# Layer 2's image attention output: fp32r products with high and low terms stacked along K instead of float32 products

## The chip, the core and the metric

The kernel runs on one core of one Trainium2 chip. The core has a matrix engine (PE), a vector engine (DVE), a scalar engine (ACT), a general engine (POOL) and a queue that issues transfers (SP); each works through its own instructions in order and waits for the others by semaphores. Sixteen DMA engines carry the transfers. The metric is the device time of one execution in microseconds, the median of several runs. Lower is better.

## The reference

Two layers of cross attention with two branches, applied one after the other to 16 sequences of 256 positions with 320 channels (20 heads of 16). Each layer attends to 252 (layer 2) or 77 (layer 1) text tokens and, beside them, to image tokens. The part that matters here is the image branch of layer 2, which has four image tokens per sequence:

```python
k_ip = heads(ip_ehs @ W_k_ip)
v_ip = heads(ip_ehs @ W_v_ip)
attn_scores = jnp.einsum('bhsd,bhnd->bhsn', q, k_ip) * attn_scale
qsem = _l2norm(jnp.einsum('bhst,bte->bhse', probs_t, text_ehs))
sem = jnp.einsum('bhse,bne->bhsn', qsem, _l2norm(ip_ehs))
probs_ip = jax.nn.softmax(attn_scores + SEM_SCALE * sem, axis=-1)
probs_ip = probs_ip * spatial_mask[None, None, :, None]
ip_out = jnp.einsum('bhsn,bhnd->bhsd', probs_ip, v_ip)
...
out = text_out + IP_SCALE * ip_out
out = out @ W_out + b_out
out = out + residual
```

The change touches `ip_out`: per sequence and head, 256 x 4 probabilities times 4 x 16 values, in float32 accuracy.

## The kernel before

The kernel runs 160 slots: 80 for layer 1, then 80 for layer 2 (`NS` = 80). A slot handles one group of four heads of one sequence ("batch"), so five slots are a batch. Work that is not attention (projections, softmax of the image branch, output projection, loading) is written as tasks, Python generators whose steps carry due times counted in slots; after certain points of a slot (`slot1` yields 0.33, 0.67 and 1.0) all steps whose time has come are issued, ordered by time and then by the order of definition. This order fixes PE's instruction stream: PE is pinned, so its queue is exactly what the program issues. The other engines and SP are ordered by a planner, which takes ready instructions, earlier-issued ones first, and inserts the semaphores. A few instructions are tied by hand: `queued` places the two operations that split the query input (L593, L594, tile `hq`) behind the last instruction of attention issued before them on ACT and POOL.

In a slot of layer 2, `both1` makes the scores of the slot after next (L891, tile S) and the transposed scores of this slot (L885, tile T); ACT takes the exponential (L905). `attend1` sums values by the probabilities (L945) and the norms (L955). `rounded1` splits the probabilities into a high part on ACT (L923) and a low part on POOL (L924); `norm1` multiplies the high part by the text tokens' Gram matrix on PE (L933) and the result by the low part's tile on DVE (L934). `norm1` has four calls per slot, of 4, 3, 4 and 3 products; tasks are issued after the first, after the third and after the fourth.

When a batch's five groups are through, task `i1` (`image_softmax`) forms the image probabilities on [128 x 160] tiles (partitions are query positions, the free axis is 8 blocks x 5 groups x 4 tokens): an inverse square root by a power on POOL (L1021), scaling and adding (L1024, L1026), the maximum, the exponential (L1033), the sum, and the normalisation (L1039, L1041). L1041 writes into a zero-padded tile `pip` [128 x 8 x 32]; DVE transposes it in 32x32 blocks to `pT` (L1048). The values stand in DRAM (`vipd`), are loaded to all 32-row blocks of `vb`, and are multiplied with a 128 x 384 0/1 mask `bmask`, so that each column of `vb` holds only its own head's group (L1049). Task `c1` (`close1`) multiplies: three float32 products of 128 x 128 by 128 x 256 (L1058), each added on DVE to the gathered text output `hT` (L1059). Then `finish` splits `hT` for the output projection (L593 to L595, tile `ho`), projects it (L605, L608) and adds bias and residual (L841, L845). The last batch's softmax runs in two parts: four groups early (task `i1a`), the fifth after the last slot.

fp32r is a 32-bit type whose products leave one record in the trace where float32 products leave two; the kernel treats it as rounded, and keeps accuracy by splitting an operand: high = the value rounded to fp32r, low = value - high rounded to fp32r, and summing high x high, high x low and low x high (`prod`, L243). L1058, like L945 and L955, is in plain float32.

Line numbers in the profile are those of the kernel before. All DMAs issued by `dma` carry L83.

Of the kernel before, what the change touches and what calls it, by code (L numbers as in the profile page):

```python
# [49 lines left out]
def xattn2(  # L50
# [80 lines left out]
    vipd = dram.tile([BI, CP], F32, name="vipd")  # L131
# [301 lines left out]
    def weights1():  # L433
# [4 lines left out]
        hop = w1["hop"] = dram.tile([128, CP], F32, name="hop")  # L438
        dma(hop, bmask_d)
# [33 lines left out]
    def weights6():  # L473
# [5 lines left out]
        vip = buf("rawc", [128, 512], bufs=2, name="vip")[:BI, :CP]  # L479
        for m in range(3):  # L480
            ms = slice(m * 128, m * 128 + 128)
            vp = bank()[:BI, :128]
            prod(vp, lambda s, k: cip[:, s, k], lambda s, k: wvi1(s, k, ms), 4)
            nc.vector.tensor_copy(vip[:, ms], vp)
            yield
# [3 lines left out]
        w1["bmask"] = f(buf("kb", [128, CP], FR, name="bmask"))  # L489
        dma(w1["bmask"], w1["hop"])  # L490
        dma(vipd, vip)
# [14 lines left out]
    def weights3():  # L506
# [500 lines left out]
    def image_softmax(b, lo=0, hi=NG):  # L1007
# [15 lines left out]
        a = small(NIP, "a")  # L1023
# [16 lines left out]
        pi = w1["pip"]  # L1040
        pool.tensor_mul(by_group(pi), a, b4(z4))  # L1041
# [6 lines left out]
        nc.vector.transpose(pT, pi.rearrange("p f c -> p (f c)"))  # L1048
        nc.vector.tensor_mul(vb, vb, w1["bmask"])  # L1049
        return pT, vb  # L1050

    def close1(b):
        hT, (pT, bd) = results["gathered", 1, b], get("i1", b)

        def extra(hT):
            for p in range(3):
                ip = bank()[:, :S]
                mm(ip, bd[:, p * 128 : (p + 1) * 128], pT, start=True, stop=True)  # L1058
# [63 lines left out]
    def shifted(n, *times):  # L1122

        return [RAMP(n + t) for t in times]
# [17 lines left out]
    for b in range(B):  # L1142
# [4 lines left out]
        task(("i1", b), shifted(n, 6.67, 6.67, 6.67, 7.33, 7.33, 7.67, 7.67, 8, 8.33), lambda b=b: image_softmax(b, NG - 1 if b == B - 1 else 0), ("gathered", 1, b), ("taken", B + b - 1), *([("i1a",)] if b == B - 1 else []))  # L1147
        task(("c1", b), shifted(n + (1.67 if b > B - 3 else 0), 8.67, 8.67, 8.67, 8.67, 9, 10.33, 11.67, 12.67), lambda b=b: close1(b), ("i1", b), ("w4", 1))
# [156 lines left out]
```

## Time and profile before

| | |
|---|---|
| median of 3 runs | 1554.69 us (1552.39 to 1557.26) |
| span of the profiled execution, first to last instruction | 1550.2 us |
| layer 2's loop | from about 800 us to 1500 us, 50.36 us a batch |
| L1058 matrix products | 96 records of 379 ns (median), first at 817.1, last at 1538.1 us |
| L1041, L1048, L1049 | 473, 434 and 546 ns (median) |

How to read the lines below. Groups and timelines name a line of the kernel, the engine, the operation, the tiles written and read, the shape and the number of instructions. In brackets stands how long the engine was idle before it and for whom it waited. PEld is PE's loading of the stationary operand; it overlaps with the products. PE's records overlap each other, so the time that PE is held is read from the chain of waits or from the distance of starts, not from the mean of a record. A float32 product leaves two records, an fp32r product one. A window of the stage table gives start:end, length, then the busy time of PE, PEld, DVE, ACT and POOL with the number of instructions, the granted clock, the DMA share and GB/s.

### The profile page before, as it was taken

The page shows a single profiled execution, that of the slowest core. Times are in us where ns is not written, and L with a number is a line of the kernel's source. Part 1 is how long each engine was busy: PE and PEld are TensorE (multiplying, and loading weights), DVE is VectorE, ACT ScalarE, POOL GpSimd, SP SyncE. Part 2 cuts the span into 40 slices and gives each one's busy share as a digit, 9 for nine tenths or more (in the row PEclk, how much of TensorE's full clock was granted, in tenths as well). Part 3 has the DMA queues.
Part 4 walks back from the last instruction along what each step waited for, and adds up shares of the span by engine and source line. Part 5 has one row for each costly group of instructions (what it writes and reads, how often), then busy time and mean ns, then how long its engine had stood idle before and what let it go on. Part 6 is the DMA issues. An engine that isn't in the chain of part 4 may idle for free.

```text
span 1550.2 us, 36017 instructions
## 1 busy us (share of the span) xinstructions
PE 1449.5 (94%) x12726; PEld 1170.2 (75%) x12726; DVE 1219.9 (79%) x2687; ACT 873.5 (56%) x1941; POOL 1196.1 (77%) x1246
## 2 busy tenths in 40 slices
PE   6789999999999989878999999999999999999996
PEld 5678888878787878656777777777777777777764
DVE  6468787778777888878777887888888888788785
ACT  5345555656564644545666666566656665666562
POOL 4259797979896976778478798878887898779786
PEclk9899999999999999989999999999999999999998
DMA  6656666676766675765354344434444444434411
GB/s 210 195 182 175 209 191 207 188 221 190 218 191 201 192 205 153 196 186 172 97 135 129 104 125 127 123 111 140 110 114 126 125 116 119 135 108 99 119 32 36
DMA packets 228815, 233.04 MB, mean 150 GB/s; under 512 B 38410, under 2 KB 198508, under 8 KB 228620
## 3 DMA queue, kind: packets, MB, share of 16 engines
q1 hardware_dynamic: 226428, 229.44, 52.0%
q8 instruction: 102, 1.67, 0.5%
q10 hardware_dynamic: 2208, 1.30, 0.3%
q14 instruction: 77, 0.63, 0.1%
HBM read 118.04 MB, written 77.10 MB: 126 GB/s over the span
## 4 chain that ended last, share of the span: by engine, by line
PE 34%; POOL 7%; DVE 7%; issue 2%; ACT 1%; DMA 1%; ACTq 1%; SPq 0%; DVEq 0%; POOLq 0%
PE X L933 11%; PE X L248 5%; POOL wt L924 5%; PE P L945 4%; PE P L955 3%; PE X L605 3%; PE T L885 2%; PE S L891 2%; DVE wt L934 2%; PE X L1058 1%; POOL hq L594 1%; DVE mn L893 1%; PE X L258 1%; DVE ho L595 1%; PE X L608 1%
## 5 line engine op out<-in xcount | busy, mean ns | idle before, releaser
L768 POOL TENSOR_TENSOR P<-P,rs 128x512 f32<-128x512 f32 x320 | 414.1, 1317 | 126.1 <-ACT P L765 125.6
L924 POOL TENSOR_TENSOR wt<-P,ctb 128x512 f32<-128x512 f32 x320 | 410.9, 1309 | 94.5 <-ACT ctb L923 91.8
L933 PE MATMUL X<-ctb,gm 128*128 128x512 f32 x1120 | 307.3, 404 | 6.0 <-DVE wt L934 5.9
L765 ACT ACTIVATE P<-T 128x512 f32<-128x512 f32 x320 | 175.9, 594 | 172.0 <-PE T L762 107.2
L934 DVE TENSOR_TENSOR wt<-X,wt 128x512 f32<-128x512 f32 x320 | 216.8, 682 | 53.3 <-PE X L933 47.8
L933 PEld LDWEIGHTS X<-ctb,gm 128*128 128x128 f32 x1120 | 196.5, 189 | 39.3 <-DVE wt L934 8.6
L905 ACT ACTIVATE P<-T 128x512 f32<-128x512 f32 x320 | 173.3, 594 | 78.8 <-PE T L885 74.6
L923 ACT ACTIVATE ctb<-P 128x512 fp32r<-128x512 f32 x320 | 187.2, 627 | 45.7 <-PE X L933 34.6
L893 DVE TENSOR_REDUCE mn<-S 128x4 fp32r<-128x1008 f32 x160 | 191.3, 1196 | 0.0
L740 DVE TENSOR_REDUCE mn<-S 128x4 fp32r<-128x716 f32 x160 | 142.3, 889 | 0.0
L795 PE MATMUL P<-P,vr 128*32 128x256 f32 x1920 | 126.9, 396 | 7.1 <-DVE tmp L812 6.7
L738 PE MATMUL S<-ks,qs 125*128 125x256 f32 x640 | 118.8, 309 | 9.2 <-DMA qs<-tph 4.6
L738 PEld LDWEIGHTS S<-ks,qs 125*128 125x128 f32 x640 | 89.3, 196 | 44.3 <-issue 23.7
L762 PE MATMUL T<-qs,ks 127*128 127x256 f32 x640 | 110.0, 293 | 4.5 <-DMA qs<-mt 2.3
L1021 POOL TENSOR_TENSOR r<-u,rs 128x40 f32<-128x40 f32 (+2 forms) x17 | 108.7, 6396 | 4.1 <-DVE u L1018 4.1
L739 DVE TENSOR_REDUCE mn<-S 128x4 fp32r<-128x308 f32 x160 | 74.2, 464 | 30.8 <-PE S L738 30.5
L762 PEld LDWEIGHTS T<-qs,ks 127*128 127x128 f32 x640 | 92.5, 198 | 7.7 <-ACT q L160 2.5
L795 PEld LDWEIGHTS P<-P,vr 128*32 128x32 f32 x1920 | 57.3, 113 | 48.6 <-issue 12.4
L806 DVE STREAM_TRANSPOSE nt<-P 128x512 f32<-128x512 f32 x80 | 56.9, 711 | 46.5 <-PE P L795 46.0
L605 PE MATMUL X<-hq,wE 128*128 128x256 f32 x512 | 80.3, 297 | 10.0 <-ACT hq L593 5.2
L945 PE MATMUL P<-P,v1t 128*32 128x256 f32 x1280 | 86.5, 388 | 0.2 <-DVE wt L934 0.2
L955 PE MATMUL P<-wt,zone 128*32 128x256 f32 x1280 | 85.3, 379 | 0.3 <-DVE wt L934 0.3
(231 smaller groups left out, 3018.0 us busy)
## 6 DMA issues: line engine op xcount, KB each, us to landing
qd<-q SPq DMA_DIRECT2D x96, 256.0 KB
qs<-tph SPq DMA_DIRECT2D x64, 308.0 KB
rawc<-in_cT_dram SPq DMA_DIRECT2D x60, 256.0 KB
qs<-qd SPq DMA_DIRECT2D x80, 192.0 KB
ks<-kd SPq DMA_DIRECT2D x80, 192.0 KB
ks<-kd SPq DMA_DIRECT2D x160, 96.0 KB
qs<-qd SPq DMA_DIRECT2D x160, 96.0 KB
kd<-kst SPq DMA_DIRECT2D x57, 256.0 KB
```

Of the source, the lines that this page charges most:

```text
L738: mm(sp[:, h], Q[: XROW + T0, h, t * 128 : (t + 1) * 128], K[: XROW + T0, h], start=True, stop=True)
L762: mm(st[p][:, j], K[:KS0, 2 * p + j, t * 128 : (t + 1) * 128], Q[:KS0, 2 * p + j], start=True, stop=True)
L765: exp = anchor(nc.scalar.activation(pt, st[p], AF.Exp, scale=SCALE))
L768: anchor(nc.gpsimd.tensor_mul(pt, pt, rs[:, t : t + 1].to_broadcast([128, 2, S])))
L795: mm(pv[32 * s : 32 * s + 32, o : o + S], v[:, vt, h : h + 32], P[k, s // 2][:, t, s % 2], start=vt < 2, stop=vt != 1,)
L893: anchor(nc.vector.tensor_reduce(maxes[k + 2][:, t], sp[:, :, :T1], axis=AX.X, op=ALU.max))
L905: anchor(nc.scalar.activation(P[k, u][:, t], st[u], AF.Exp, scale=SCALE))
L923: nc.scalar.activation(R[k, u][:, t], P[k, u][:, t], AF.Copy, scale=0.5)
L924: anchor(nc.gpsimd.tensor_sub(W[k, u][:, t], P[k, u][:, t], f(R[k, u][:, t])))
L933: mm(yp, gm[:, gb], R[k, u][:, kt], start=i == 0, stop=i == len(blocks[n]) - 1)
L934: nc.vector.tensor_mul(W[k, u][:, n], yp, W[k, u][:, n])
L945: mm(pv[32 * s : 32 * s + 32, :S], v[:, n, h : h + 32], P[k, s // 2][:, n, s % 2], start=n == 0, stop=n == 1 and not before,)
```

## The change

The probabilities and the values are both split in a high and a low part, and the three partial products are stacked along the contraction axis of one fp32r product:

- A 32-column block of `pip` held five groups x 4 tokens of one block of positions. Now it holds two groups x four terms x 4 tokens: the terms of the probabilities are high, high, low and zero. Five groups need three blocks (groups 0 and 1, 2 and 3, 4), in two tiles: 512 columns for the first two, 256 for the last.
- `vipd` holds four terms of the values per batch to match: high, low, high, high. They are made once, in `weights6`, with a copy on ACT and a subtraction on DVE per 128 columns, and written with four DMAs.
- `image_softmax` multiplies in place (`a`), then copies the high part on ACT (three copies), copies it again to the second term (three copies on ACT) and subtracts for the low part on POOL (three subtractions). Groups 0 to 3 have 64 elements a partition and operation, group 4 has 32. This is a step of its own with a due time of 8.
- DVE transposes the two tiles (512 and 256 columns) into a scratch tile `turned`, and two DMAs on SP bring them to the fp32r tile `pT` (128 x 768).
- Each of the three products now takes its own third of `pT`.
- The 128 x 384 mask from DRAM gives way to a 128 x 24 mask `own`, built on the chip, broadcast over 16 columns; its DRAM copy (`hop`) goes.
- The due times of `c1`'s first five steps move from 8.67, 8.67, 8.67, 8.67, 9 to 9, 9, 9, 9, 9.33.

```diff
-    vipd = dram.tile([BI, CP], F32, name="vipd")
+    vipd = dram.tile([B, 4, NIP, CP], F32, name="vipd")
...
-        hop = w1["hop"] = dram.tile([128, CP], F32, name="hop")
-        dma(hop, bmask_d)
...
-        vip = buf("rawc", [128, 512], bufs=2, name="vip")[:BI, :CP]
+        vip = [buf("rawc", [128, 512], bufs=2, name="vip")[:BI, :CP] for i in range(2)]
...
-            nc.vector.tensor_copy(vip[:, ms], vp)
+            nc.scalar.copy(vip[0][:, ms].bitcast(FR), vp)
+            nc.vector.tensor_sub(vip[1][:, ms].bitcast(FR), vp, vip[0][:, ms])
...
-        w1["bmask"] = f(buf("kb", [128, CP], FR, name="bmask"))
-        dma(w1["bmask"], w1["hop"])
-        dma(vipd, vip)
+        kb = buf("kb", [128, 4 * S - 128], FR, name="pT")
+        w1["pT"], w1["vb"] = kb[:, : 3 * S], buf("M", [128, CP], FR, bufs=SIZES["M"], name="vb")
+        w1["own"] = f(kb[:, 3 * S : 3 * S + 24])
+        own = kb[:, 3 * S : 3 * S + 24].rearrange("p (a s r) -> p a s r", a=3, s=4)
+        nc.gpsimd.memset(w1["own"], 0.0)
+        for s in range(4):
+            nc.gpsimd.memset(f(own[32 * s : 32 * s + 32, :, s]), 1.0)
+        even, odd = tmask[:, 4:5], tmask[:, 6:7]
+        nc.vector.tensor_scalar_mul(own[:, :, :, 0], f(own[:, :, :, 0]), even)
+        nc.vector.tensor_scalar_mul(own[:, 2, :, 1], f(own[:, 2, :, 1]), even)
+        nc.vector.tensor_scalar(own[:, :2, :, 1], f(own[:, :2, :, 1]), odd, -1.0, op0=ALU.mult, op1=ALU.mult)
+        for t, s in enumerate((0, 1, 0, 0)):
+            dma(vipd[:, t], vip[s])
...
-            w1["vb"], w1["mhalf"] = one[:, :CP], one[:, CP : CP + NG * 8]
-            w1["pT"], w1["pip"] = two[:, :S], two[:, S:].rearrange("p (f c) -> p f c", c=32)
+            w1["pip"], w1["mhalf"] = (one, two[:, :S]), two[:, S : S + NG * 8]
             nc.vector.memset(w1["mhalf"], -0.5)
-            nc.gpsimd.memset(w1["pip"], 0.0)
+            for t in w1["pip"]:
+                nc.gpsimd.memset(t, 0.0)
...
+            w1["turned"] = buf("nt", [128, 2 * S], bufs=2, name="turned")
...
-        a = small(NIP, "a")
+        a_all = buf("a", [128, NG, 8, NIP])
+        a = a_all[:, gs]
...
         pool.tensor_mul(z4, z4, mk.unsqueeze(1).to_broadcast([128, n, 8]))
-        pi = w1["pip"]
-        pool.tensor_mul(by_group(pi), a, b4(z4))
+        pool.tensor_mul(a, a, b4(z4))
+        yield
+        parts = []
+        for i, r, of in ((0, 0, (0, 2)), (0, 1, (1, 3)), (1, 0, (4,))):
+            if lo <= of[0] < hi:
+                x = w1["pip"][i].rearrange("p (x r t n) -> p x r t n", r=2, t=4, n=NIP)[:, :, r]
+                parts.append((x, a_all[:, of[0] : of[-1] + 1 : 2]))
+        for x, src in parts:
+            nc.scalar.copy(x[:, :, 0].bitcast(FR), src)
+        for x, src in parts:
+            nc.scalar.copy(x[:, :, 1], x[:, :, 0])
+            pool.tensor_sub(x[:, :, 2].bitcast(FR), src, x[:, :, 0])
         if hi < NG:
             return
         vb = w1["vb"]
-        dma(vb, vipd[NIP * b : NIP * (b + 1)].unsqueeze(0).to_broadcast([32, NIP, CP]))
+        dma(vb, vipd[b].rearrange("t n c -> (t n) c").unsqueeze(0).to_broadcast([8, 4 * NIP, CP]))
         yield
         pT = w1["pT"]
-        nc.vector.transpose(pT, pi.rearrange("p f c -> p (f c)"))
-        nc.vector.tensor_mul(vb, vb, w1["bmask"])
-        return pT, vb
+        for at, x in zip((pT[:, : 2 * S], pT[:, 2 * S :]), w1["pip"]):
+            turned = w1["turned"] if at.shape[1] > S else buf("both", [128, S], bufs=2, name="turned")
+            nc.vector.transpose(turned, x)
+            dma(at, turned)
+        blocks = lambda t: t.rearrange("p (x e) -> p x e", e=16)
+        nc.vector.tensor_mul(blocks(vb), blocks(f(vb)), w1["own"].unsqueeze(2).to_broadcast([128, 24, 16]))
+        return pT.rearrange("p (a q) -> p a q", a=3), vb
...
-                mm(ip, bd[:, p * 128 : (p + 1) * 128], pT, start=True, stop=True)
+                mm(ip, bd[:, p * 128 : (p + 1) * 128], pT[:, p], start=True, stop=True)
...
-        task(("i1", b), shifted(n, 6.67, 6.67, 6.67, 7.33, 7.33, 7.67, 7.67, 8, 8.33), lambda b=b: image_softmax(
+        task(("i1", b), shifted(n, 6.67, 6.67, 6.67, 7.33, 7.33, 7.67, 7.67, 8, 8, 8.33), lambda b=b: image_softmax(
...
-        task(("c1", b), shifted(n + (1.67 if b > B - 3 else 0), 8.67, 8.67, 8.67, 8.67, 9, 10.33, 11.67, 12.67), lambda b=b: close1(b)
+        task(("c1", b), shifted(n + (1.67 if b > B - 3 else 0), 9, 9, 9, 9, 9.33, 10.33, 11.67, 12.67), lambda b=b: close1(b)
```

More of the change, by code (lines that the diff above doesn't have):

```diff
@@ L1146, in xattn2 @@
         task(("o1", b), shifted(n, -7.67, -7, -6.67, -5.33, -4.33, -4), lambda b=b: open1(b), ("w7",), ("c0", b), *([("o1", b - 1)] if b else []))
-        task(("i1", b), shifted(n, 6.67, 6.67, 6.67, 7.33, 7.33, 7.67, 7.67, 8, 8.33), lambda b=b: image_softmax(b, NG - 1 if b == B - 1 else 0), ("gathered", 1, b), ("taken", B + b - 1), *([("i1a",)] if b == B - 1 else []))
-        task(("c1", b), shifted(n + (1.67 if b > B - 3 else 0), 8.67, 8.67, 8.67, 8.67, 9, 10.33, 11.67, 12.67), lambda b=b: close1(b), ("i1", b), ("w4", 1))
+        task(("i1", b), shifted(n, 6.67, 6.67, 6.67, 7.33, 7.33, 7.67, 7.67, 8, 8, 8.33), lambda b=b: image_softmax(b, NG - 1 if b == B - 1 else 0), ("gathered", 1, b), ("taken", B + b - 1), *([("i1a",)] if b == B - 1 else []))
+        task(("c1", b), shifted(n + (1.67 if b > B - 3 else 0), 9, 9, 9, 9, 9.33, 10.33, 11.67, 12.67), lambda b=b: close1(b), ("i1", b), ("w4", 1))
     task(("i1a",), [2 * NS + 0.1], lambda: image_softmax(B - 1, 0, NG - 1), ("i1", B - 2))
```

## The prediction

> **What bounds the kernel now.** I read the first page for the shares, then layer 2 alone (the only part that the change touches while the kernel is in its loop), then the chain of waits through one of its batches, then the waits of the same stretch.
>
> ```profile
> span 1550.2 us, 36017 instructions
> PE 1449.5 (94%) x12726; PEld 1170.2 (75%) x12726; DVE 1219.9 (79%) x2687; ACT 873.5 (56%) x1941; POOL 1196.1 (77%) x1246
> ```
> ```profile
> 1200.00:1400.00 200.00, 197.78 (x1759) 153.88 (x1758) 165.77 (x356) 125.73 (x271) 164.08 (x181) 1.00 0.44 120
> ```
>
> The second fence is 200 us of layer 2: PE 197.78 us busy, weight loads 153.88, VectorE (DVE) 165.77, ScalarE (ACT) 125.73, GpSimd (POOL) 164.08, clock 1.00. PE is nearly full, DVE and POOL have a sixth to spare on average. Averages hide the place that matters, and the chain of waits shows it: once in every batch it leaves PE.
>
> ```profile
> 1261.20 2.39 POOL wt L924 x2
> ...
> 1263.70 0.29 POOL z L1039
> ...
> 1264.06 0.47 POOL rs L1041
> 1264.53 2.21 POOL wt L924 x2
> ...
> 1266.98 1.31 POOL hq L594
> ...
> 1268.34 1.10 PE X L605 x7
> 1269.44 1.64 PE X L933 x7
> 1271.08 1.30 PE X L1058 x6
> 1272.37 0.70 PE X L933 x3
> 1273.07 0.43 PE S L891 x4
> ...
> 1288.64 0.94 PE X L605 x8
> ```
> ```profile
> 1210.84 2.44 POOL wt L924 x2
> ...
> 1311.56 2.39 POOL wt L924 x2
> ```
> ```profile
> PEld S L891 <- DVE hT L1059: 4.8, 13, 0.4
> PEld X L605 <- POOL hq L594: 4.5, 13, 0.5
> ```
>
> Columns of the chain: start, length, what. From 1261.20 to 1268.3 the chain runs on POOL, through the end of the image softmax (L1039, L1041) and the low halves of the next query input (L594), and only then back to PE, which had to wait for L594. The same place recurs at 1210.84 and 1311.56: two batches in 100.72 us, 50.36 a batch. The waits (total us, times, longest) say that this wait occurs 13 times, 0.35 us each. So in 13 of the 16 batches POOL and PE are in balance there to a third of a microsecond: a microsecond more on POOL ahead of L594 lengthens the batch by that much, and a microsecond less on PE behind it (L1058 stands there) shortens it by that much.
>
> **The change, part by part.**
>
> *The products.* The six records of L1058 (three float32 products, two records each) take 1.30 us of the chain, 0.217 each. L605 has fp32r products with the same 128x256 moving tile, one record each: eight in 0.94, 0.118 each. Three of those are 0.35, so PE gains 0.95 us a batch.
>
> *The low terms on POOL.* What was one multiply into the padded tile (L1041) becomes a multiply in place of the same size, and three subtractions (64, 64 and 32 elements a partition) come after it.
>
> ```profile
> 1532.85 0.41 POOL L1031 TENSOR_TENSOR a<-a,m 128x128 f32<-128x128 f32 x1
> ...
> 1533.30 0.31 ACT L1033 ACTIVATE a<-a 128x128 f32<-128x128 f32 x1 [5.58 <-POOL a L1031]
> ...
> 1534.10 0.24 POOL L1031 TENSOR_TENSOR a<-a,m 128x32 f32<-128x32 f32 x1 [0.30 <-DVE m L1029]
> 1534.37 0.23 ACT L1033 ACTIVATE a<-a 128x32 f32<-128x32 f32 x1 [0.77 <-POOL a L1031]
> ```
>
> A POOL operation with 32 elements takes 0.24, with 128 it takes 0.41; 64 by the straight line between them is 0.30, so 0.30 + 0.30 + 0.24 = 0.84 us (bounds: three times 0.24 = 0.72, and 0.41 + 0.41 + 0.24 = 1.06). In the program these are issued right after L1041's step and before the step with L594, at the same due time 8; when the two L924 end (1266.74), their inputs are there (next item). I place them ahead of L594 and cost them in full: PE, which waits for L594 already, waits 0.84 longer.
>
> *The copies on ACT.* Six small ones, 0.23 to 0.31 each by the two ACT rows above, 1.5 us in all. They can start after L1041 (1264.53).
>
> ```profile
> 1264.45 1.08 ACT L905 ACTIVATE P<-T 128x512 f32<-128x512 f32 x2
> 1266.56 1.09 ACT L905 ACTIVATE P<-T 128x512 f32<-128x512 f32 x2 [1.03 <-PE T L885]
> ```
>
> ACT has L905 until 1265.53 and then 1.03 us idle. The first three (0.75), on which the subtractions wait, fit there and are done by 1266.3, while POOL works on its two L924: no wait on POOL. The other three push the next L905 back by about 0.45; behind it lie two casts, L913's copy of the maxima and its DMA, needed only by the next slot's products, which themselves come later. Costed at nothing; 0.45 a batch if that cover is gone.
>
> *The transposes on DVE.* One of 256 goes, one of 512 and one of 256 come: 0.71 us more by the row of layer 1.
>
> ```profile
> L806 DVE STREAM_TRANSPOSE nt<-P 128x512 f32<-128x512 f32 x80 | 56.9, 711 | 46.5 <-PE P L795 46.0
> ```
> ```profile
> 1268.36 0.68 DVE L934 TENSOR_TENSOR wt<-X,wt 128x512 f32<-128x512 f32 x1
> ...
> 1270.18 0.69 DVE L934 TENSOR_TENSOR wt<-X,wt 128x512 f32<-128x512 f32 x1 [0.94 <-PE X L933]
> ```
>
> Their input is complete at 1266.98 + 0.84 = 1267.8; behind the L934 at 1268.36 they run from about 1269.05 to 1270.2, in the 0.94 us that DVE idled there. Nothing for DVE itself; 0.71 without that gap.
>
> *The two new DMAs.* Each transposed tile goes by the SP queue from SBUF to SBUF into pT, 256 KB and 128 KB. The trace has no such transfer. The nearest are sd (80 KB, 1.62 us as a link of the chain) and the image values (192 KB, issued 1526.42, used by L1049 at 1529.14: at most 2.72).
>
> ```profile
> 1500.76 1.62 DMA sd<-sq
> ```
> ```profile
> 1526.42 0.57 SPq L83 DMA_DIRECT2D rs<-vipd  x1
> ...
> 1529.14 0.56 DVE L1049 TENSOR_TENSOR rs<-rs,kb 128x384 f32<-128x384 f32 x1
> ```
> ```profile
> 1268.31 0.38 SPq L83 DMA_DIRECT2D xq<-x1d  x1
> 1269.73 0.49 SPq L83 DMA_DIRECT2D rawc<-in_cT_dram  x1
> ```
>
> Issued at 1269.8 and 1270.25 they land between 1271.4 and 1273.0. PE comes to the products at 1271.08 + 0.84 + 0.70 = 1272.6 (L933's three now go first, see below). So it waits between nothing and 0.4 us; I take 0.2. On SP they may find the context load of 1269.73 ahead of them, which waits for POOL and so comes 0.84 later; then 0.7 more. The Trainium skill's page "DMA: Bandwidth & Descriptors" (Anatomy of one DMA) states, for another issuing path, about 2.0 us fixed and the bytes at 436 GB/s. By that, an estimate from the page, the tiles would land 2.6 and 2.3 us after issue, and the wait would be nearly nothing; the 1.62 us link for 80 KB lies below its 2.2, so the trace does not follow it exactly.
>
> *The moved steps.* The products go from due time 8.67 to 9, which is behind L933's last three products of the slot and just ahead of L891's scores. With them move the three additions (L1059), the load of the residual, and by as much the halves of hT (L593 to L595, 9 to 9.33), whose consumer stays at 10.33: a whole slot (50.36 / 5 = 10 us) of cover remains. The row "S L891 <- DVE hT L1059" shows that the scores take a PSUM space that the work just before must drain. After the change the work just before is L933's last product, drained by an L934, of which the trace shows:
>
> ```profile
> 1273.18 0.69 DVE L934 TENSOR_TENSOR wt<-X,wt 128x512 f32<-128x512 f32 x1 [0.28 <-PE X L933]
> ```
>
> That is 0.28 + 0.69 = 0.97 after L933 ends, and the products fill 0.35 of it: a wait of up to 0.6 for L891, or none if the spaces fall differently. I take 0.4, about the 0.37 of the waits' row.
>
> *Once.* Four small DMAs instead of three, three ACT copies, the mask and a larger zero fill come in; they lie in the change of layers and off the chain. Nothing, at most 1.5 us (three copies of the ACT rows' size and a DMA issue of 0.5 by the SP rows).
>
> *The tail.* In the last batches nothing covers the new latency.
>
> ```profile
> 1524.83 1.56 PE X L1058 x6
> ...
> 1535.70 0.46 DVE rs L1048
> ...
> 1536.19 2.94 PE X L1058 x6
> ...
> 1539.67 0.84 ACT ho L593
> ```
> ```profile
> 1524.44 5.44 POOL L1021 TENSOR_TENSOR r<-u,rs 128x32 f32<-128x32 f32 x1
> ```
>
> Batch 15: from 1535.7, where the one transpose stood, come a copy (0.23), a subtraction (0.24), two transposes (1.15), three hand-overs (0.05 each) and a DMA (1.6 to 2.7), so the last product starts at 1539.0 to 1540.1 and L593, behind a product and its addition (0.7), at 1539.7 to 1540.8 instead of 1539.67: I take 0.7. Batch 14 feeds the same chain at 1524.83: a copy (0.25), the subtractions (0.84), a longer transpose (0.71) and a DMA (2.15, the middle) make its products 3.95 later and the products are 0.95 shorter, and since PE issues in order, what follows them is 3.0 later. If its subtractions queue behind the power at 1524.44 (5.44 us), it is 8. I take 0.7 + 3.0 = 3.7 (1 to 9).
>
> *Sum.* A balanced batch: -0.95 + 0.84 + 0.2 + 0.4 = +0.49; 13 of them +6.4. Batch 13 has no L594 behind it: -0.95 + 0.6 = -0.35. Tail +3.7. Together +9.7 on the profiled 1550.2, 1559.9; the runs' median (1554.69) lies 4.5 above that span, so 1564.
>
> **The rivals.**
>
> *PE's gain stays.* POOL's order is the planner's, not the program's; should the subtractions come behind L594 and the scores find free space, a batch is 0.95 shorter: 14 x -0.95 + 3.7 = -9.6, 1545. For it: L594 is held only behind the L924 and everything else on POOL moves freely, and nothing needs pT before 1272. Against it: the subtractions are issued first and are ready.
>
> *Balance.* POOL's 0.84 is paid, the two waits taken at 0.6 are not: 13 x -0.11 - 0.95 + 3.7 = +1.3, 1556. For it: both waits are bounded by nothing from below.
>
> *A new wait decides.* If the planner puts the subtractions directly behind L1041, POOL, which issues in order, waits for ACT until 1266.3, and the two L924 and L594 behind come up to 1.8 later; or the pT loads stand behind the context load (0.7). With 1.0 a batch more, +13, and the tail near its upper end, +4: 1581. Against it: before L1039, where ACT and DVE had to answer, the planner filled POOL with two L924 (1261.20).
>
> That the change does not do what it says is excluded by L605: fp32r products of that shape do run in one record of 0.118.
>
> **How the numbers follow.** Forecast 0.42, gain stays 0.28, balance 0.13, a new wait 0.17. A measurement of this kernel tells 0.3% (4.7 us) from no change: below 1550.0 is faster, above 1559.4 slower. Faster is the first rival, 0.28 (its own spread reaches little above 1550). Same is the balance and some of the forecast's lower end, 0.16. Slower is the rest, 0.56. The forecast's own range is 1557 to 1572; for 8 in 10 I go down to 1543 and up to 1580.
>
> **What would show it.** Right: three L1058 records a batch at 0.12; three POOL subtractions of 0.2 to 0.35 between L1041 and L594; L605 waiting for L594 near 1.2 us instead of 0.35; period near 50.85; the last products after 1539. Wrong: L594 ahead of the subtractions and a period near 49.4 (first rival); L605's wait unchanged; POOL idle behind L1041, or L1058 waiting for the pT load by a microsecond (third rival).

## The result and the profile after

| | before | after |
|---|---|---|
| median, four runs each on one chip | 1555.61 us (1552.39 to 1557.26) | 1574.23 us (1568.55 to 1583.78) |
| span of the profiled execution | 1550.2 us | 1571.6 us |
| ratio after / before | | 1.0131, 95% interval 1.0092 to 1.0171 |

The changed kernel is slower by 0.9 to 1.7%. Lines of the kernel after stand 9 to 25 higher than before: L594 (`hq`) is now L603, L605 L614, L891 L900, L924 L933, L933 L942, L934 L943, L1021 L1031, L1041 L1051, L1048 L1071, L1049 L1074, L1058 L1083 and L1059 L1084. L1059 and L1061 are now the copies on ACT, L1062 the subtractions on POOL.

The long power of the image softmax (L1021, now L1031) runs once a batch and is a good clock. Counted from its starts, the 21.4 us of the two spans lie here:

| stretch | before | after | difference |
|---|---|---|---|
| start to the power of batch 2 | 894.3 | 890.2 | -4.1 |
| eleven batches of the loop | 554.6 (50.42 each) | 567.5 (51.59 each) | +12.9 |
| batch 13 to batch 14 | 45.6 | 45.9 | +0.3 |
| last long power to the end | 55.7 | 68.0 | +12.3 |

The first row is layer 1 and the change of layers. In the kernel before with nothing but a due time changed, the same point came at 900.2 in one profiled execution; I read no cost or gain out of it. What has to be explained are 1.17 us a batch and 12.3 us at the end.

The stage table for the stretch that the prediction quoted, after:

```profile
1200.00:1400.00 200.00, 191.68 (x1688) 148.18 (x1687) 164.93 (x346) 124.13 (x285) 162.89 (x185) 0.99 0.45 127
```

PE is no longer full: 191.68 us of 200 instead of 197.78, and DVE and POOL are no busier (164.93 and 162.89, before 165.77 and 164.08). From 900 to 1400 us PE was busy 493.93 us of 500 before and 479.34 after; with the periods above that is 49.81 us busy and 0.61 idle in a batch before, 49.46 busy and 2.13 idle after. So PE's work became a little shorter and its idle time grew by 1.5 us a batch. The chain of waits through one batch shows where (start, length, what):

```profile
1265.92 2.41 POOL wt L933 x2
...
1268.43 0.28 POOL z L1050
...
1268.78 0.47 POOL a L1051
1269.26 2.49 POOL wt L933 x2
1271.75 1.25 POOL hq L603
1273.00 0.58 POOL rs L1062 x2
...
1273.60 0.72 DVE nt L1071
...
1274.34 2.85 DMA kb<-nt
...
1277.23 0.83 PE X L1083 x3
1278.06 0.43 PE S L900 x4
```

Up to L603 it is the chain of before. There it went to PE; now it stays on POOL for the subtractions (L1062), which stand *behind* `hq` and not ahead of it, goes to DVE for the transpose, and then to the new transfer of 2.85 us from SBUF to SBUF, for which PE waits with the three products. The waits of PE from 800 to 1515 us (total us, times, longest) after:

```profile
PE X L1083 <- DMA kb<-nt: 13.0, 13, 2.8
...
PE X L942 <- DVE wt L943: 10.0, 10, 1.4
...
PEld X L614 <- POOL hq L603: 4.7, 13, 0.6
```

and one row of the same view of before:

```profile
PE X L933 <- DVE wt L934: 5.9, 12, 0.8
```

The wait for `hq` is what it was (4.7 us after, 4.5 before, in 13 batches). New is PE's wait for the load of `pT`: 2.8 us in the first batch of layer 2, then 0.2 to 1.9, in the mean 0.85. The wait for DVE's L943 has also grown. On the SP queue a 384 KB load of the next query input (`xq`) was issued 1.3 us ahead of this load, in this and in most other batches. Where the chain of the loop passes this load, in ten batches, it takes 2.73 to 3.94 us; at the end of the kernel, where nothing had been issued for 22 us, the same transfer took 2.32.

At the end of the kernel, the chain after:

```profile
1533.56 5.43 POOL r L1031
1538.99 0.58 POOL rs L1062 x2
...
1540.33 2.32 DMA kb<-nt
...
1542.69 1.02 PE X L1083 x3
...
1543.74 4.37 DMA M<-vipd
...
1548.13 0.56 DVE M L1074
1548.69 1.01 DVE hT L834 x3
...
1550.58 1.66 POOL r L1031
...
1555.84 3.95 DMA kb<-both
...
1559.92 0.57 PE X L1083
```

The subtractions of batch 14 stand behind the 5.43 us power of batch 15's first part. Its products start 9.1 us after that power started (before: 1524.83 - 1524.44 = 0.4). Then comes something that no step of the prediction names: the image values of batch 15 are loaded into the one tile `vb`, so the load starts when batch 14's products have read it (1543.74), takes 4.37 us (in the kernel before it was issued behind them too, at 1526.42, but DVE did not wait for it), and DVE works in order: the mask multiply (L1074), which waits for that load, stands ahead of the transposes L834 on which the last part depends. From the power with 32 elements (1533.56) to the last one (1550.58) there are 17.0 us; before it was 1531.23 - 1524.44 = 6.8. Behind the last power, the 128 KB load takes 3.95 us and the way to L593's successor L602 (1560.96) takes 10.4 instead of 8.4. That load was not alone either: the load of the residual, 384 KB, was issued on the same queue 0.49 us ahead of it.

```profile
1555.35 0.37 SPq L83 DMA_DIRECT2D xc<-x1d  x1
1555.84 0.48 SPq L83 DMA_DIRECT2D kb<-both  x1
```

In three other runs this last load takes 3.55, 2.67 and 2.40 us with the residual's issue 0.62, 0.83 and 1.25 us ahead (e3_old_due, f3_mask, e2_late). In f3_mask and e2_late the same 128 KB of batch 14, with nothing issued in the 5 us before, take 1.95.

### The profile page after: what moved, and what is told of

The parts are those of the page before. It is cut to its first block, busy times and chain, and to the rows that moved or that the text cites. A ratio compares the mean times of both kernels' runs of the same rounds, so it can differ in the third digit from the quotient of the medians.

```text
span 1571.6 us, 36137 instructions
## 1 busy us (share of the span) xinstructions
PE 1439.7 (92%) x12678; PEld 1153.9 (73%) x12678; DVE 1231.3 (78%) x2706; ACT 887.2 (56%) x2040; POOL 1207.6 (77%) x1300
## 5 line engine op out<-in xcount | busy, mean ns | idle before, releaser
L933 POOL TENSOR_TENSOR wt<-P,ctb 128x512 f32<-128x512 f32 x320 | 409.7, 1307 | 80.7 <-ACT ctb L932 79.6
L942 PE MATMUL X<-ctb,gm 128*128 128x512 f32 x1120 | 300.8, 400 | 10.1 <-DVE wt L943 10.0
L943 DVE TENSOR_TENSOR wt<-X,wt 128x512 f32<-128x512 f32 x320 | 214.8, 678 | 35.6 <-PE X L942 30.1
L942 PEld LDWEIGHTS X<-ctb,gm 128*128 128x128 f32 x1120 | 195.5, 189 | 43.8 <-DVE wt L943 12.3
L902 DVE TENSOR_REDUCE mn<-S 128x4 fp32r<-128x1008 f32 x160 | 191.4, 1196 | 0.0
L804 PE MATMUL P<-P,vr 128*32 128x256 f32 x1920 | 130.8, 407 | 3.4 <-DVE tmp L821 3.4
L1031 POOL TENSOR_TENSOR r<-u,rs 128x40 f32<-128x40 f32 (+2 forms) x17 | 108.7, 6394 | 4.1 <-DVE u L1028 4.1
L964 PE MATMUL P<-wt,zone 128*32 128x256 f32 x1280 | 88.7, 390 | 0.5 <-DVE wt L943 0.5
L614 PE MATMUL X<-hq,wE 128*128 128x256 f32 x512 | 79.2, 294 | 10.8 <-ACT hq L602 5.5
```

The costliest lines, as they stand in the source:

```text
L804: mm(pv[32 * s : 32 * s + 32, o : o + S], v[:, vt, h : h + 32], P[k, s // 2][:, t, s % 2], start=vt < 2, stop=vt != 1,)
L902: anchor(nc.vector.tensor_reduce(maxes[k + 2][:, t], sp[:, :, :T1], axis=AX.X, op=ALU.max))
L933: anchor(nc.gpsimd.tensor_sub(W[k, u][:, t], P[k, u][:, t], f(R[k, u][:, t])))
L942: mm(yp, gm[:, gb], R[k, u][:, kt], start=i == 0, stop=i == len(blocks[n]) - 1)
L943: nc.vector.tensor_mul(W[k, u][:, n], yp, W[k, u][:, n])
```

## The experiments

Twelve runs, in three groups. The table collects what the profiled execution of each shows: the mean period over eleven batches, the median of these eleven batches, PE's busy and idle time in the mean batch (from the busy time between 900 and 1400 us), the stretch from the last long power to the end, then the median of all its runs and the ratio to the kernel before on the same chip (its medians there: 1551.37 to 1551.92).

| run | period | median batch | busy | idle | end | median time | ratio (95%) |
|---|---|---|---|---|---|---|---|
| before | 50.42 | 50.36 | 49.81 | 0.61 | 55.7 | 1555.61 | |
| after | 51.59 | 51.50 | 49.46 | 2.13 | 68.0 | 1574.23 | 1.0131 (1.0092 to 1.0171) |
| e1_act_copy | 51.56 | 51.55 | 49.13 | 2.43 | 62.6 | 1574.78 | 1.0140 (1.0097 to 1.0183) |
| e2_late | 50.93 | 50.85 | 49.29 | 1.63 | 69.2 | 1565.36 | 1.0086 (1.0054 to 1.0117) |
| e3_old_due | 52.97 | 52.97 | 50.16 | 2.81 | 66.9 | 1591.87 | 1.0248 (1.0210 to 1.0287) |
| e4_before_due9 | 51.52 | 51.33 | 49.86 | 1.66 | 56.6 | 1570.53 | 1.0092 (1.0064 to 1.0120) |
| f1_before_due9_mask | 50.21 | 50.24 | 49.86 | 0.35 | 56.3 | 1548.62 | 1.0005 (0.9980 to 1.0030) |
| f2_act_copy_mask | 50.39 | 50.43 | 49.20 | 1.18 | 62.6 | 1556.90 | 1.0045 (1.0025 to 1.0066) |
| f3_mask | 51.56 | 51.28 | 49.44 | 2.12 | 65.7 | 1573.60 | 1.0168 (1.0134 to 1.0202) |
| f4_act_copy_mask_tie | 50.61 | 50.44 | 49.26 | 1.35 | 59.4 | 1556.79 | 1.0040 (1.0014 to 1.0065) |
| g1_vb | 50.58 | 50.42 | 49.22 | 1.37 | 56.7 | 1556.32 | 1.0022 (0.9997 to 1.0048) |
| g2_vb_933 | 49.89 | 49.86 | 49.23 | 0.65 | 56.8 | 1550.87 | 0.9987 (0.9964 to 1.0011) |
| g3_vb_967 | 50.58 | 50.60 | 49.37 | 1.21 | 57.2 | 1559.78 | 1.0036 (1.0006 to 1.0065) |
| g4_products_only | 50.87 | 50.41 | 49.04 | 1.83 | 55.9 | 1552.20 | 1.0010 (0.9985 to 1.0035) |

In several profiled executions single batches are 1.3 to 2.1 us longer than their neighbours (52.49 among 50.4 in g1_vb, three of 52 among 50.4 in g4_products_only). What makes them was not taken apart; the mean periods contain them, the medians of the batches hardly do. The line numbers of the runs differ by a few: L1049 is L1054 and L1058 is L1063 in f1_before_due9_mask; L924, L933, L934, L891 and L1058 are L925, L934, L935, L892 and L1066 in g4_products_only; in f4_act_copy_mask_tie and the runs g1 to g3 L1062 is L1064, L1074 is L1081 and L1083 is L1090.

### First group: the load and the moved due time, each alone

**e1_act_copy**: the changed kernel with the transposed tiles copied to `pT` by ACT instead of a transfer.

```diff
-            dma(at, turned)
+            nc.scalar.copy(at, turned)
```

> The changed kernel with the two transposed tiles brought to pT by copies on ACT instead of DMAs. Theory A (PE waits for the pT load, 1.28 us in each of 12 batches, and what is behind it is late with it): the batch falls from 51.6 to 50.3 or below, the tail from the last power to the end loses the two loads (2.3 and 3.95 us) less two copies, and the time is about 1574 - 16 - 4 = 1554. Theory B (the copies on ACT, the longer transposes on DVE and the moved due times cost it, the load only shows it): the batch stays above 51.2, the loop gains less than 5 us.

**e4_before_due9**: the kernel before with the due times of the change alone.

```diff
-    ... 8.67, 8.67, 8.67, 8.67, 9, 10.33, 11.67, 12.67), lambda b=b: close1(b), ...
+    ... 9, 9, 9, 9, 9.33, 10.33, 11.67, 12.67), lambda b=b: close1(b), ...
```

> The kernel before with the moved due times of the change alone (products at 9, float32, no load). Theory A: the batch stays within 0.2 of 50.36 and the total within 0.3%. Prediction's scores wait: the scores behind the products wait for the drain of the products' predecessor, a batch is 0.3 to 0.6 longer, total up to +8.

Both results are as large as the whole loss of the loop: without the load the period is still 51.56, and the kernel before, moved by a third of a slot and otherwise untouched, has 51.52. So there are two causes, each of which is enough. The waits of PE in e1_act_copy:

```profile
PEld X L942 <- DVE wt L943: 23.3, 12, 2.0
PE X L942 <- DVE wt L943: 20.8, 12, 1.8
```

and in e4_before_due9:

```profile
PEld X L933 <- DVE wt L934: 21.2, 14, 2.0
PE X L933 <- DVE wt L934: 18.3, 12, 1.8
```

In both, PE waits 1.5 to 1.7 us a batch for DVE's drain of the Gram products (before 5.9 us in all). The groups of instructions show what made DVE late (count | busy us, mean ns). Before, then e4_before_due9:

```profile
L1049 DVE TENSOR_TENSOR rs<-rs,kb 128x384 f32<-128x384 f32 x10 | 5.5, 546 | 0.0
```
```profile
L1049 DVE TENSOR_TENSOR rs<-rs,kb 128x384 f32<-128x384 f32 x10 | 16.4, 1642 | 0.0
```

The same multiply of the values with the mask, same shape, takes three times as long. The timeline of e4_before_due9 around it:

```profile
1287.96 3.16 POOL L924 TENSOR_TENSOR wt<-P,ctb 128x512 f32<-128x512 f32 x2
1288.48 1.50 DVE L595 SCALAR_TENSOR_TENSOR ho<-ho,tmask,hT 128x256 fp32r<-128x256 f32 x1
...
1289.90 1.64 DVE L1049 TENSOR_TENSOR rs<-rs,kb 128x384 f32<-128x384 f32 x1
...
1295.64 0.96 PE L933 MATMUL X<-ctb,gm 128*128 128x512 f32 x3 [1.46 <-DVE wt L934]
```

It runs from 1289.90 to 1291.54, beside the second of two L924 on POOL that follow each other without a pause and take 3.16 us instead of 2.5. In the kernel before it ran at 1277.14, between one L924 that ended at 1276.93 and the next at 1277.69. L595, just ahead of it, is no part of the difference: it stood beside an L924 before too (1508 ns there, 1507 here). The Trainium skill's page "SBUF — State Buffer" (SBUF: two separate sides) says that a VectorE operation with two SBUF inputs and a GpSimd operation that reads SBUF lock each other out of a shared port for the whole instruction. The rows agree with that: the multiply, which met no L924 before, gets 1.1 us longer and ends 0.42 us after the L924 that it meets. The 0.7 of the pair lie mostly in its first L924 (1.73 us), beside L594 and L595; the kernel before has an L924 of 1.74 us there.

### Second group: both causes apart and together

The mask multiply, with the load before it, becomes a step of its own with a due time in the middle of the batch, `queued` behind DVE's last attention instruction, where nothing waits for it:

```diff
-        vb = w1["vb"]
-        dma(vb, vipd[...]...)
+        vb = get("vm", b)
...
-        nc.vector.tensor_mul(...)
...
+    def masked(b):
+        vb = w1["vb"]
+        dma(vb, vipd[...]...)
+        yield
+        queued(nc.vector.tensor_mul(...))
+        return vb
...
+    for b in range(B):
+        task(("vm", b), [NS + 5 * b + (4.6, 6.4)[b == B - 1], NS + 5 * b + (5.4, 6.6)[b == B - 1]], lambda b=b: masked(b), *([("taken", B + b - 1)] if b else []))
```

**f1_before_due9_mask**: e4_before_due9 with this step.

> The kernel before with the moved due times, and with the mask multiply L1049 taken out of the image softmax into a task of its own, tied to a place in the fifth slot of the batch where POOL is idle. Theory C (the moved due time pushes L594, L595 and L1049 on DVE into POOL's L924, L1049 takes 1.64 us instead of 0.55, and PE waits for L934 behind it): the mask multiply is back near 0.55 us, a batch falls from 51.33 to 50.4 or below, PE's wait for L934 from 1.66 to 0.6, total 1553 to 1558. Theory D (the place of the products ahead of the scores costs it): a batch stays at 51.3.

```profile
L1054 DVE TENSOR_TENSOR rs<-rs,kb 128x384 f32<-128x384 f32 x10 | 5.6, 563 | 0.0
```
```profile
PEld X L933 <- DVE wt L934: 4.2, 12, 0.4
```

The multiply is back at 563 ns, the wait of PE's weight loads at 4.2 us (21.2 in e4_before_due9), the period at 50.21, and the median level with the kernel before. That shows that the whole cost of the moved due time was the mask multiply at this place: L595 is as long as ever (1508 ns), and the median batch falls by 1.09 us, as much as the meeting had added to the multiply. The step takes the multiply away altogether and its load with it, so that the added time and not the multiply itself made the loss is argued from these two numbers, not shown alone.

**f2_act_copy_mask** (e1_act_copy with the step) and **f3_mask** (the changed kernel with the step and with its load):

> The changed kernel with copies on ACT for the load of pT and the mask multiply in a task of its own. Theory C: with both waits gone a batch is 50.3 or below (51.55 with the copies alone), total 1555 to 1560, what is left is in the tail. Theory B: a batch stays above 51.2.

> The changed kernel with the load of pT by DMA, and the mask multiply in a task of its own. Theory C (two waits, each enough by itself, side by side): PE still waits 1.2 us or more for the load at the products, a batch is 50.9 to 51.5; if the load were no cause, it would be 50.3 as with the copies.

With the load kept, next to nothing is gained (51.56, 1573.60; the median batch 51.28 against 51.50). In the changed kernel as it stands, L1074 takes 1578 ns in one batch of ten and 543 to 557 in the others: the batch is already late by the load, and the multiply misses the POOL operations. With both removed the period is 50.39 and the ratio falls from 1.0131 to 1.0045. The two waits hid behind each other; either alone keeps nearly the full loss. What is left of the first in f2_act_copy_mask is a short wait for the copies on ACT (2.6 us of PE's time in 11 batches).

**e2_late** and **e3_old_due**: the changed kernel with its products at due times 9.67 and 8.67.

```diff
-    ... 9, 9, 9, 9, 9.33, ...
+    ... 9.67, 9.67, 9.67, 9.67, 10, ...        (e2_late)
+    ... 8.67, 8.67, 8.67, 8.67, 9, ...         (e3_old_due)
```

> The changed kernel with the products due two thirds of a slot later (9.67, halves of hT at 10), so that the load has some 6 us more. Theory A: PE no longer waits for the load, a batch is near 50.0, about 1558. Theory B: a batch stays above 51.2.

> The changed kernel with the due times of before (8.67 ... 9). Theory A: PE comes to the products about 0.7 us earlier (ahead of the three products of L942) and waits that much longer, a batch is 52 to 52.5, total about 1574 + 7. Theory B, as far as it is the moved due time: a batch falls below 51.2.

The earlier PE asks for `pT`, the more it loses: period 52.97, 51.59 and 50.93 for 8.67, 9 and 9.67. In e3_old_due PE waits 23.0 us for the load's first tile in 13 waits and another 1.9 for the second. In e2_late PE does not wait for the load at all in the loop, and another wait has come, that of the scores behind DVE's reduction of the maxima:

```profile
PE S L900 <- DVE mn L902: 14.8, 13, 1.2
```

So with this design the due time 9 is better than the old one, which would cost another 1.1%; 9.67 is better still by the medians (1565.36 against 1574.23), though the intervals of the two ratios overlap.

### Third group: the end, and where PE's gain goes

**f4_act_copy_mask_tie**: f2_act_copy_mask with the last power placed behind the low terms of batch 14.

```diff
+        power = pool.tensor_tensor(r, u, ..., op=ALU.pow)
+        if hi < NG:
+            queued(power, w1["low"])
...
+            w1["low"] = pool.tensor_sub(x[:, :, 2].bitcast(FR), src, x[:, :, 0])
```

> As f2, and the power of the last batch's four groups (5.44 us on POOL) tied behind the low terms of the batch before it. If the tail's loss is that the low terms stand behind that power: the products of batch 14 come some 5 us earlier, and the time from the last long power (6.8 us) to the end falls by 4 to 6 us against f2, total 1550 to 1555. If the tail's loss is only the added steps: no more than 1 us.

**g1_vb**: the same with a tile of its own for the image values of batch 15. Its mask step is due at the same place as in the other batches (4.6 and 5.4 instead of 6.4 and 6.6) and no longer waits for batch 14.

```diff
-        vb = w1["vb"]
+        vb = w1["vb"] if b < B - 1 else buf("cta", [128, 2, 512], FR, bufs=SIZES["CTA"], name="vbl")[:, 0, :CP]
```

> The changed kernel with pT by ACT copies, the mask multiply in a step of its own, the last power behind the low terms, and the image values of batch 15 in a tile of their own, so that their load waits for no product. Theory (the tail's remainder is that load): the 3.56 us load and the mask multiply behind it leave the chain, the stretch from the last long power to the end goes from 59.4 to about 56.3 (that of the kernel before with the same mask step), the period stays at 50.44, total about 3 us below the 1556.8 of the version with one tile: 1553 to 1554. Rival (DVE's hT work is late for another reason): the stretch stays at 59 and the total at 1557.

The stretch from the last long power to the end goes 68.0 (after), 62.6 (no load of `pT`), 59.4 (low terms first), 56.7 (own tile); before it is 55.7. The 3.2 us of the second step are less than the 4 to 6 expected. From the power with 32 elements to the last one: 17.0, 14.4, 8.5 and 6.9, before 6.8. In f4_act_copy_mask_tie the chain still has the values' load and the mask multiply:

```profile
1528.20 0.71 PE X L1090 x3
1528.92 3.56 DMA M<-vipd
...
1532.51 0.76 DVE M L1081
```

In g1_vb it goes through POOL alone from the subtractions to the power:

```profile
1529.43 0.55 POOL rs L1064 x2
1529.97 0.23 POOL hsn L1014
1530.21 0.21 POOL rs L1064
1530.42 0.16 POOL u L1026
1530.58 5.43 POOL r L1031
```

That settles the end in the traces, one profiled execution each and in this order: the load of `pT`, the order on POOL and the one tile `vb` make up 5.4, 3.2 and 2.7 of its 12.3 us. The medians do not show the last two steps (1556.90, 1556.79, 1556.32): 3 us is less than these intervals can tell, and both profiled executions had longer batches in the loop.

**g4_products_only**: f1_before_due9_mask with three fp32r products of the high terms alone. The low terms are left out, so POOL has no subtraction; ACT makes one copy of 256 elements.

```diff
-        nc.vector.transpose(pT, pi.rearrange("p f c -> p (f c)"))
+        turned = buf("both", [128, S], bufs=2, name="turned")
+        nc.vector.transpose(turned, pi.rearrange("p f c -> p (f c)"))
+        nc.scalar.copy(pT, turned)
```

(`pT` and `vb` are fp32r tiles here.)

> The kernel before with due time 9 and the mask step (1548.6 us, period 50.24, PE busy 99.3% of the loop), and three fp32r products of the high terms alone in place of three float32 products; the low terms are left out, so POOL has no subtraction and ACT only one copy of 256 elements more. Theory A (a microsecond less on PE shortens the batch): the period falls by up to 0.95 to 49.3 to 49.7, the total by 8 to 13 us to 1536 to 1541. Rival B (POOL's round is the next bound, and lies just under 50.24): the period stays at 50.0 to 50.2 and the total at 1546 to 1549; then the low terms cost what the products cannot gain.

PE's microsecond is worth nothing here: the median batch takes 50.41 us against 50.24 in f1_before_due9_mask, and the median time is level with the kernel before. The same place in both traces, f1_before_due9_mask first:

```profile
1214.43 2.49 PE L933 MATMUL X<-ctb,gm 128*128 128x512 f32 x10
...
1216.37 1.35 DVE L934 TENSOR_TENSOR wt<-X,wt 128x512 f32<-128x512 f32 x2
...
1216.76 1.46 PE L1063 MATMUL X<-rs,rs 128*128 128x256 f32 x6
...
1218.14 0.50 PE L891 MATMUL S<-ks,qs 48*128 48x256 f32 x4
```
```profile
1219.68 2.49 PE L934 MATMUL X<-ctb,gm 128*128 128x512 f32 x10
...
1221.79 1.28 DVE L935 TENSOR_TENSOR wt<-X,wt 128x512 f32<-128x512 f32 x2
...
1222.01 0.52 PE L1066 MATMUL X<-kb,M 128*128 128x256 f32 x3
...
1223.12 0.50 PE L892 MATMUL S<-ks,qs 48*128 48x256 f32 x4 [0.59 <-DVE wt L935]
```

In the first, six records of float32 products stand between the last Gram product and the scores, and DVE needs just that time to drain: the scores follow without a gap, 3.71 us after the Gram products began. In the second, three short records leave the drain uncovered: the scores wait 0.59 us for L935 and begin 3.44 us after them. From the second batch to the thirteenth it is the same: a wait of 0.59 to 0.90 where f1_before_due9_mask has none. Of the 0.95 us only 0.27 is left here, and it goes in the slots behind, where PE waits 6.8 us in 12 batches for L935 (0.7 in f1_before_due9_mask). So at due time 9 the long products had been the cover of DVE's work. Why DVE is later in the slot behind was not taken apart; two of its operations there take longer than in f1_before_due9_mask, L595 (`ho`, 1174 ns against 1039) and L596 (`hq`, 722 against 528). The rival, POOL's round, is not excluded as a second limit: the chain passes the long power on POOL in six batches of layer 2's loop here, in two in f1_before_due9_mask and in none in the kernel before. And no run has the three short products at the due time of before without the load, so for that place it is not shown that the microsecond is worth nothing.

**g2_vb_933** and **g3_vb_967**: g1_vb with the products at 9.33 and 9.67, and the mask step moved by 0.2 and 0.6 of a slot to stay behind the products of the batch before.

> As the run with a tile of its own for batch 15, with the products at due time 9.33 and the halves at 9.67, a third of a slot later. Theory A (the 0.95 us that PE gained is given back in waits just ahead of and behind the products: PE is busy 49.25 of 50.42 us a batch, the products wait 0.95 a batch for pT and L942 0.88 for DVE): with the operands early the period falls to 49.5 to 49.8, and the total by 14 x 0.8 to about 1543, under the kernel before by 0.5%. Rival B (POOL, which carries 0.82 us more a batch, is the bound now): the period stays at 50.4 and the total at 1553.

> The same with the products at due time 9.67 and the halves at 10. Theory A: the period is that of the run at 9.33 or lower by the rest of the pT wait, unless the halves now come late for their consumer at 10.33, as the waits for L594's and L902's work in the run without the mask step let one suspect (1.8 us a batch there): then 50.2 to 50.8 and 1550 to 1558. Rival B: 50.4 as at the other due times.

At 9.33 the period is 49.89, half a microsecond below that of the kernel before, with the work of the change complete. Between 900 and 1400 us:

```profile
900.00:1400.00 500.00, 493.44 (x4399) 380.41 (x4392) 413.96 (x902) 332.79 (x761) 415.40 (x481) 1.00 0.43 123
```

So POOL, with the same instructions in 49.89 us, is not the bound at 50.4 that the rival supposed. It may be the next one: the chain passes the long power in eleven batches of g2_vb_933, and L933 and the power make up 34% of it between 900 and 1400 us, where L924 makes up 9% in the kernel before. Nor is all of the gain surely PE's: at 9.33 the halves of `hT` come free of most of POOL's L933 (L603 and L604 take 692 and 479 ns, 934 and 1511 in g1_vb), and no run has the products of before at that due time. The step from batch 13 to 14 takes 48.8 us there, against 43.9 in f1_before_due9_mask, which gives back 4.9 of the gain. The chain passes there through the copy of `pT` on ACT, a transfer that ACT issues behind it (`qs`, 3.29 us) and an L604 of 1.50; whether these are the cause was not tested. The median is 1550.87 and its ratio, 0.9987 (0.9964 to 1.0011), cannot be told from the kernel before. At 9.67 the scores wait for the maxima again (L902, 7.8 us), and the period is 50.58. No version run here beats the kernel before by more than the measurement can tell.

## Why the prediction was right or wrong

The forecast was 1564 (1543 to 1580), slower the likeliest; the time was 1574. The sign was right, the sum of +9.7 about half of the +21.4 between the spans, and most of its terms were wrong. The narrower range of the forecast itself, 1557 to 1572, missed. That the time lies inside the wider one owes more to luck than to the mechanism: a wait that was forecast at `hq` did not come, and others that were not forecast came in its place. Two of the signs that the prediction had named for being wrong appeared: the wait of L605 (now L614) for `hq` unchanged, and products that wait for the load.

- *The products* (-0.95 us): the size was right, three records follow each other in 0.36 to 0.38 us in the chain of g2_vb_933. That "a microsecond less on PE behind it shortens it by that much" was wrong: PE's busy time falls by 0.6 to 0.8 us a batch in the runs with copies on ACT at due times 9 and 9.33 and in g4_products_only, but with the products alone the period does not follow at due time 9. The step took PE's wait for L594 as the only place in a batch where the chain leaves PE. The same chain of the kernel before leaves it a second time in the batch shown, for DVE's drain, among the lines that the prediction passes over between 1273.07 and 1288.64:

```profile
1281.21 0.61 DVE wt L934
...
1281.87 0.97 PE X L933 x3
```

So PE and DVE were in balance there already: 5.9 us of waits in 12 batches before, against 4.5 in 13 for L594. At due time 9 without the long products there is another such place, the scores right behind them.
- *The low terms on POOL* (+0.84): they take 0.82 us, but not where the step put them. "I place them ahead of L594 and cost them in full" failed: the planner put them behind it, and the wait for `hq` did not change (4.7 us against 4.5). That was the condition of the first rival; its gain did not come, for the reason in the next point but one.
- *The copies and transposes*: next to nothing of them shows in a wait (POOL's subtractions wait twice for a copy, 0.7 us in all); the first transpose runs at 1273.60, right behind the subtractions it needs.
- *The two new DMAs* (+0.2): this is where more than half of the loop's loss lies in the changed kernel, 13.0 us of PE's waits in 13 batches, 2.8 in the first and 0.85 in each of the others. The normalisation (L1041, now L1051) came at 1264.06 before and at 1268.78 after, 4.72 later in the clock of the trace. With that shift the step's times were good: issue at 1269.8, measured 1274.34 - 4.72 = 1269.6; landing between 1271.4 and 1273.0, measured 1277.19 - 4.72 = 1272.5. What was wrong is when PE gets there: the step let PE come 0.84 late, behind a delayed `hq`. As `hq` was not delayed, PE stood at the products that much earlier, and the load, which depends on the same subtractions, did not come earlier with it. So the 0.84 was paid after all, at the next place at which PE needs POOL's result. The third rival's sign, products that wait for the load "by a microsecond", is what the trace shows; neither of its mechanisms is (POOL does not wait for ACT behind L1051, and the load is issued at once). The estimate from the Trainium skill's page "DMA: Bandwidth & Descriptors" (Anatomy of one DMA), 2.6 us for the 256 KB tile, lies between the 2.73 to 3.94 of the loop and the 2.32 of the end; for the 128 KB tile it gives 2.3, and the last one took 3.95. What the step expected ahead of the tiles on SP was the context load; it was the load of the next query input in the loop, and that of the residual at the end.
- *The sum of a batch* (+0.49): these terms, -0.95 + 0.85, would leave it level. But PE's busy time fell by only 0.35 in the changed kernel (its L1083 records have a median of 356 ns there, 280 in g2_vb_933, where they do not wait), and of the 1.5 us more of idle time about two thirds of a microsecond are not the load but mostly waits for DVE (L943), which the step did not have. Together 1.17.
- *The moved steps* (+0.4): alone they cost 1.10 us a batch (e4_before_due9; 0.97 by the median batch), and by another mechanism. The wait of the scores that this step names, "up to 0.6", is the 0.59 of g4_products_only, so it exists, but it stands in the changed kernel behind the longer one for the load. In the changed kernel the load's wait covers this cost, as f3_mask shows. What the move does by itself is to bring DVE's L1049, which runs behind the halves of `hT`, beside an L924 of POOL. The step costed the halves at nothing because their consumer has a slot of cover; it looked at the consumer and not at what the work behind them on DVE then meets on POOL.
- *Once*: nothing to see in a start that varies by some microseconds.
- *The tail* (+3.7): it was 12.3. Batch 14's part was 3.0, "8 if its subtractions queue behind the power", and they did; the path from power to power grew by 10.2. The whole is above the upper bound of 9. The 2.7 us that g1_vb recovers were in no bound: the load into the one tile `vb`, and the transposes behind it on DVE. Batch 15's part was 0.7 and came to 1.9, with a transfer of 3.95 us, the residual's load just ahead of it, where 1.6 to 2.7 was assumed.

## What to carry to other kernels

Shortening the busiest engine is worth only what its neighbours leave: look at what drains its results in the next microsecond, since a long instruction may be the cover of another engine's work. When one wait is removed and the time stays, look for a second of the same size behind it, and remove both before judging either. When steps move, check for every one of them, and for the work behind it, which operation on the other engine it will now meet. Price a transfer between two tiles of SBUF by what is issued on its queue just ahead of it: here 1.95 us (128 KB) and 2.32 us (256 KB) with nothing ahead, and up to 3.95 us behind a 384 KB load.

## What the runs showed of the hardware

- One DVE multiply of 128 x 384 with both inputs in SBUF took 546 to 563 ns in the mean when it met no L924 on POOL and 1642 ns beside one in ten of ten batches of e4_before_due9. How much it costs depends on how the two lie: in e2_late, beside the same operation, it took 579 to 730 ns. The halves of `hT` show the same: L604 takes 479 ns in g2_vb_933 and 1507 in the changed kernel (1508 in the kernel before), L603 692 and 1279.
- A transfer from SBUF to SBUF on the SP queue took 2.32 us for 256 KB and 1.95 for 128 KB with nothing issued in the 5 us before. With a 384 KB load issued shortly before on the same queue it took longer: 2.79 to 3.94 us for 256 KB with 1.3 us between the two, and 3.95, 3.55, 2.67 and 2.40 us for 128 KB with 0.49, 0.62, 0.83 and 1.25 us between them. Whether the two share the engines or stand in line was not taken apart.
- Where PE was idle for long stretches the granted clock was lower: 0.78 from 1510 us to the end in the changed kernel and 0.86 before, against 0.99 and 1.00 in the loop; from 1555.3 to 1559.9, with no product at all, it was 0.50.
